# A block-routed expert layer: second matmul in 32x32 blocks, its output turned by VectorE instead of TensorE, and some first loads reordered

## The chip, the core and the metric

The kernel runs on one core of a Trainium2 chip. The core has a matrix engine (TensorE, PE in the profile; its weight loads are the row PEld), a vector engine (VectorE, DVE), a scalar engine (ScalarE, ACT), a general engine (GpSimd, POOL) and SyncE (SP), which here only asks for transfers. Transfers run on 16 DMA engines and are asked for by SP or POOL. Matrix products read SBUF and write PSUM; DVE and ACT read both, and what they copy from PSUM to SBUF is called an eviction here. The metric is device time in microseconds of one execution, the median of several.

## What is computed

`x` and the context are 4 x 1024 x 512, fp32. A layer norm and a cross-attention with 16 heads of 32 are added to `x`; after a second layer norm comes the expert layer, which is the part most touched by the change. Cut to what matters:

```python
grouped = x.reshape(B, g, t, d)                         # 128 groups of t = 32 tokens
logits  = einsum('bgtd,des->bgtes', grouped, controller) + tie   # 32 x 4 = 128 experts
perm    = (logits == max(logits, over t))               # each expert takes one token of a group
dispatched   = einsum('bgtd,bgtes->bgesd', grouped, perm)
inner        = relu(einsum('bgesd,desf->bgesf', dispatched, f1) + bias)   # f = 32
intermediate = einsum('bgesf,esfd->bgesd', inner, f2)   # back to d = 512
out          = einsum('bgesd,bgtes->bgtd', intermediate, perm)
```

So every one of 128 experts has its own 512x32 and 32x512 matrices and sees one token of each of the 128 groups. The second layer is thus 128 small products: 128 groups x 32 hidden times 32 x 512. Its result is needed with the experts on the contraction axis, since the last line sums over experts: for one group, (32 tokens x 128 experts) times (128 experts x 512).

## The kernel before, in words

**Attention** (`attention_phase`, to line 1409) works in 16 units (4 batches x 4 groups of 4 heads). A planner written in Python (`post`, `choose`, `run_engines`, `columns`) gives each piece of work a cost and lays out a fixed order for PE, DVE, ACT, POOL and SP. Before the planner starts, lines 1028 to 1056 issue the first unit by hand: on SP the first 128 columns of the weights for keys, values and queries, the first context and rows, then (lines 1036 to 1042) the other 384 columns of each weight (`load_others`), the output weight (`load_weight("o")`), and the biases `bo_sb` and `bv_sb`. `bv_sb` is spread by a DVE copy (line 1074) that stands in DVE's order ahead of the centring of rows 4 to 7 (line 251).

**First expert layer** (`FirstLayer.dispatch`, line 1457, and `products`, line 1544). For each quarter `c` of the 512 columns, `dispatch` multiplies rows by the 0/1 matrix, so that `disp` holds [128 columns, 128 experts, 128 groups]; `products` multiplies by `f1` and adds into `inner`, which holds [4 experts x 32 hidden, 32 sets of 4 experts, 128 groups]. Weights come in blocks of 512 KB through a pool of four buffers (`load_weights`, `next_weights`): 16 blocks of `f1`, then 16 of `f2`.

**Second expert layer** (from line 1595). The 512 output columns are worked in `DQ` = 4 slices of `DW` = 128. In each slice:

- `second_layer` (line 1612), called for `m` = 0 to 7: 16 products, each of one expert, with `inner` as the stationary operand: 32 hidden x 128 groups, times 32 x 128 of `f2`. Four experts lie on the four groups of 32 partitions and write four PSUM tiles `py`, with the groups on the partitions. Four evictions (line 1608 on DVE, 1610 on ACT) write them into `y` [128 groups, 128 columns, 128 experts].
- `turn` (line 1633), called for `k` = 0 to 31: four 128x128 transposes on PE take a column's [groups, experts] to [experts, groups]; one eviction of each four, DVE and ACT by turns, writes `yT` [128 experts, 128 groups, 128 columns].
- `combine` (line 1650), called for `a` = 0 to 7 in the loop of the following slice, between the products of that slice: 16 products `po` of `permT` (one group's 128 experts x 32 tokens) with `yT`, a DVE addition to the rows of `x` (line 1661), and a store of 256 KB, mostly asked for by POOL.

`permT` (2 MB) is loaded once, the rows of `x` in 32 loads of 256 KB, both on SP. The order of PE, DVE, ACT and SP in this part is that of the program text (`manual_schedule`); an instruction that waits holds up all behind it on its engine.

Of the kernel before, what the change touches and what calls it, by code (L numbers as in the profile page):

```python
# [18 lines left out]
P = 128  # L19
# [13 lines left out]
def attention_phase(  # L33
# [1001 lines left out]
    load_ctx(0, 1)  # L1035
    for key, src in (("q", wqT), ("k", wkT), ("v", wvT)):
        load_others(key, src)
    load_weight("o", woT)
    bo_sb = opool.tile([P, D], F32, tag="bo", name="bo_sb")
# [7 lines left out]
    ln_root(0)  # L1047
    run(v_step(0, 0))
    for t in range(4):
        ln_center(t)  # L1050
# [4 lines left out]
    ln_root(1)  # L1055
    run(q_step(0, 0))
    even = wpool.tile([P, 32], F32, tag="even", name="even")
    nc.gpsimd.memset(even, 1.0 / D)
# [353 lines left out]
class FirstLayer:  # L1412
# [44 lines left out]
    def dispatch(self, c, n, rows, disp, banks=None):  # L1457
        nc = self.tc.nc
        T, G = self.T, self.G
        half, tb = divmod(n, 4)  # L1460
        disp_v = disp[:, :, ts(half, G // 2)].rearrange("p e (r t) -> p r e t", r=4)
        pool, tag = banks or (self.ps_d, "pd")
        pds = [
            pool.tile([P, 4, self.ES], F32, tag=tag, name=f"pd_{c}_{n}_{r}") for r in range(4)
        ]
        for i in range(4):
            for r in range(4):
                nc.tensor.matmul(  # L1468
                    pds[r][:, i, :], lhsT=rows(i)[ts(r, T), :],
                    rhs=self.perms[ts(r, T), 4 * n + i, :], start=True, stop=True,  # L1470
                )
        for r in range(4):
            dst = disp_v[:, r, :, ts(tb, 4)]
            src = pds[r].rearrange("p t e -> p e t")
            if r % 2 == 0:
                nc.vector.tensor_copy(dst, src)
            else:
                nc.scalar.copy(dst, src)
# [3 lines left out]
def ffn_phase(ctx: ExitStack, tc, consts, x2_dram, routed, first_layer, f1, biasT, f2, out):  # L1482
# [25 lines left out]
    wpool = pool(ctx, "ffn_w", 4, side="right")  # L1508
    DQ, NM = f2.shape[0], f2.shape[1]
    DW = D // DQ  # L1510
    weights = deque()

    def load_weights(n):


        w = wpool.tile([P, 8 * P], F32, tag="w", name=f"w_{n}")
        if n < 4 * NC:
            c, k = divmod(n, 4)
            nc.sync.dma_start(w, f1[ts(c, P), ts(k, 8 * P)])
        else:  # L1520
            dq, k = divmod(n - 4 * NC, NM // 2)
            w = w.rearrange("p (m i d) -> p m i d", m=2, i=4)
            nc.sync.dma_start(w, f2[dq, ts(k, 2)].rearrange("m p i d -> p m i d"))
        weights.append(w)

    for n in range(4):
        load_weights(n)
    loads = iter(range(4, 4 * NC + DQ * NM // 2))

# [7 lines left out]
    with first_layer.stack:  # L1537
# [6 lines left out]
        def products(c, disp, f1k, k):  # L1544
            pi = ps_i.tile([P, QB, G], F32, tag="pi", name=f"pi_{c}_{k}")
            for q in range(QB):
                nq = k * QB + q
                for j in range(4):
                    nc.tensor.matmul(  # L1549
                        pi[ts(j, F), q, :],  # L1550
                        lhsT=f1k[:, ds(((k % 2 * QB + q) * 4 + j) * F, F)],
                        rhs=disp[:, 16 * (nq // 4) + 4 * j + nq % 4, :],
                        start=True, stop=True,
                    )
# [40 lines left out]
    with ExitStack() as second:  # L1595
        ytpool = pool(second, "ffn_yT", 1)
        xpool = pool(second, "ffn_x", 8)
        tpool = pool(second, "ffn_permT", 1)
        ypool = pool(second, "ffn_y", 1)
        ps_y = pool(second, "ps_y", 6, space=PSUM)  # L1600
        ps_o = pool(second, "ps_o", 2, space=PSUM)
        permT = tpool.tile([ES, N], F32, tag="permT", name="permT")
        x2_v = x2_dram.rearrange("(a t p) d -> a p t d", p=P, t=4)
        out_v = out.rearrange("(a t p) d -> a p t d", p=P, t=4)

        def evict(on_vector, dst, src):
            if on_vector:
                nc.vector.tensor_copy(dst, src)
            else:
                nc.scalar.copy(dst, src)  # L1610

        def second_layer(dq, m, y):

            f2t = weights[0][:, m % 2]

            banks = [(ps_y, "py")] * 3 + [(ps_o, "po") if dq == 0 else (ps_y, "py")]
            pys = [
                pool.tile([G, 4, DW], F32, tag=tag, name=f"py_{dq}_{m}_{j}")
                for j, (pool, tag) in enumerate(banks)
            ]  # L1620
            for i in range(4):
                for j in range(4):
                    nc.tensor.matmul(  # L1623
                        pys[j][:, i, :], lhsT=inner[ts(j, F), 4 * m + i, :],
                        rhs=f2t[ts(j, F), i, :], start=True, stop=True,
                    )
            for j in range(4):
                evict(
                    j == 0 or (j == 2 and (dq == 0 or m == NM - 1)), y[:, :, ds(16 * m + 4 * j, 4)],
                    pys[j].rearrange("g i d -> g d i"),  # L1630
                )

        def turn(dq, k, y, yT):

            pt = ps_y.tile([ES, 4, G], F32, tag="py", name=f"pt_{dq}_{k}")
            for i in range(4):
                nc.tensor.transpose(pt[:, i, :], y[:, 4 * k + i, :], ident)  # L1637
            evict(k % 2 == 0, yT[:, :, ts(k, 4)], pt.rearrange("e i g -> e g i"))

        xts = deque()  # L1640
        rows = iter([(dq, a) for dq in range(DQ) for a in range(NM)])

# [7 lines left out]
        def combine(dq, a, yT):  # L1650

            xt = xts.popleft()
            po = ps_o.tile([P, 4, DW], F32, tag="po", name=f"po2_{dq}_{a}")
            for i in range(4):
                t = 4 * a + i
                for r in range(4):
                    nc.tensor.matmul(  # L1657
                        po[ts(r, T), i, :], lhsT=permT[:, ds(t * P + r * T, T)],
                        rhs=yT[:, (t // 16) * GH + r * 16 + t % 16, :], start=True, stop=True,
                    )  # L1660
# [3 lines left out]

        yT = None
        with tc.manual_schedule(engines=order):
            for dq in range(DQ + 1):
                before = yT
                if dq < DQ:
                    y = ypool.tile([G, DW, ES], F32, tag="y", name=f"y_{dq}")  # L1670
                for m in range(NM):
                    if dq < DQ:
                        second_layer(dq, m, y)
                        if m % 2 == 1:
                            weights.popleft()
                            next_weights()
                    if dq:
                        combine(dq - 1, m, before)
                        if m < NM - 1:
                            load_x()  # L1680
                    elif m == 1:
                        nc.sync.dma_start(permT, permT_dram)
                if dq < DQ:
                    yT = ytpool.tile([ES, G, DW], F32, tag="yT", name=f"yT_{dq}")
                    for k in range(DW // 4):
                        turn(dq, k, y, yT)
                        if k % 4 == 3 and (dq == 0 or k == 3):
                            load_x()

# [66 lines left out]
```

## Time and profile before

| what | value |
|---|---|
| median of the timed runs | 1349.78 us (1345.71, 1350.24, 1349.78) |
| the profiled execution's own time, its span | 1340.95 us, 1339.2 us |
| granted TensorE clock, mean | 0.992 |
| busy share of the span: PE, PEld, DVE, ACT, POOL | 96%, 50%, 67%, 36%, 37% |
| second expert layer, first `py` product to the end | 1198.6 to 1339.2 us |
| first product `py` (line 1623) to last | 1198.6 to 1309.2 us, 1024 records |
| turns `pt` (line 1637) | 1211.0 to 1324.7 us, 512 records |
| combines `po` (line 1657) | 1230.9 to 1333.4 us, 1024 records |
| DMA in the whole span | 119.59 MB, mean 89 GB/s |

An fp32 product shows as two records of PE, a transpose as one. A group line of the profile reads: line, engine, operation, what it writes <- what it reads, shapes, xcount | busy us, mean ns of one | idle us of its engine just before, and what ended that idle. A timeline line reads: start us, duration us, engine, line, operation, and in brackets the idle before it and its releaser; neighbours of one kind are merged into one line. A window line gives a stretch, its length, the busy time of PE, PEld, DVE, ACT and POOL with counts, the granted clock, the busy share of the DMA engines and GB/s.

### The profile page before, as it was taken

Reading aid. Unit: us, or ns where it says so; the run is one execution under the profiler, and the core shown is the slowest. Engines: PE = TensorE matmul, PEld = TensorE weight load, DVE = VectorE, ACT = ScalarE, POOL = GpSimd, SP = SyncE. Lnnn points to the kernel's source line nnn. Section 1 sums busy time; section 2 is a strip of 40 time slices with the busy share of each in tenths; the row PEclk is TensorE's granted clock in tenths of the full one; section 3 lists DMA queues with packets and bytes.
Section 4 is the critical chain, followed back from the end, with each engine's and each line's share of the span. In section 5 each row is a group of like instructions: output and inputs, shape, how many; then the busy total and the mean of one; then the engine's idle time right before and its main releaser. Section 6 shows DMA issues by size and latency. Waiting matters only on the chain.

```text
span 1339.2 us, 45912 instructions
## 1 busy us (share of the span) xinstructions
PE 1280.7 (96%) x20926; PEld 666.2 (50%) x20926; DVE 891.5 (67%) x1189; ACT 487.1 (36%) x694; POOL 497.1 (37%) x683
## 2 busy tenths in 40 slices
PE   7999999999999999999999999999997999998997
PEld 3533453345344534443434344444532556788887
DVE  5675756766676678566667666676676566776776
ACT  1123333343333333333323233333344234456663
POOL 1036365655242435734252437152564110000211
PEclk9999999999999999999999999999998999998999
DMA  8101202110130211002311010010313776655665
GB/s 291 34 2 59 85 17 69 36 44 14 57 122 27 72 53 54 26 22 79 102 41 53 25 30 12 20 36 26 99 58 108 271 223 200 198 162 189 205 206 144
DMA packets 87730, 119.59 MB, mean 89 GB/s; under 512 B 7128, under 2 KB 48496, under 8 KB 87408
## 3 DMA queue, kind: packets, MB, share of 16 engines
q1 hardware_dynamic: 84656, 107.22, 25.2%
q0 software_dynamic: 2880, 9.44, 2.2%
q8 instruction: 163, 2.67, 0.8%
q14 instruction: 31, 0.25, 0.1%
HBM read 87.33 MB, written 29.31 MB: 87 GB/s over the span
## 4 chain that ended last, share of the span: by engine, by line
PE 81%; DVE 9%; issue 4%; DMA 3%; POOL 1%; SPq 1%; ACT 1%; DVEq 0%; POOLq 0%
PE sc L588 11%; PE pk L27 8%; PE pq L27 8%; PE av L832 8%; PE pv L27 7%; PE st L726 7%; PE po L27 6%; PE pt L1637 4%; PE st L719 3%; PE pd L1468 3%; PE pi L1549 2%; PE po L1657 2%; PE py L1623 2%; PE po L1300 2%; DVE nm L607 2%
## 5 line engine op out<-in xcount | busy, mean ns | idle before, releaser
L735 ACT ACTIVATE pr<-st 128x1024 f32<-128x1024 f32 (+1 forms) x320 | 282.8, 936 | 453.4 <-PE st L726 392.8
L743 POOL TENSOR_SCALAR_AFFINE_SELECT pr<-pr 128x256 f32<-128x256 f32 x256 | 130.0, 525 | 378.5 <-ACT pr L735 372.8
L617 DVE TENSOR_REDUCE nm<-sc 128x2 f32<-128x1024 f32 x192 | 226.1, 1219 | 48.4 <-PE sc L588 27.1
L811 POOL TENSOR_TENSOR acc<-acc,pr 128x256 f32<-128x256 f32 (+3 forms) x122 | 189.6, 1565 | 62.8 <-ACT pr L735 56.1
L811 DVE TENSOR_TENSOR acc<-acc,pr 128x1024 f32<-128x1024 f32 (+3 forms) x128 | 125.9, 998 | 80.8 <-POOL pr L743 48.8
L588 PE MATMUL sc<-kT,qT 32*128 32x512 f32 (+3 forms) x1536 | 170.2, 523 | 0.4 <-DVE qT L423 0.2
L832 PE MATMUL av<-pr,v 128*32 128x512 f32 (+3 forms) x1536 | 158.2, 495 | 5.6 <-POOL pr L743 5.0
L726 PE MATMUL st<-qT,kT 32*128 32x512 f32 (+3 forms) x1536 | 154.9, 489 | 0.0
L27 PE MATMUL pk<-ct,w_k 128*32 128x512 f32 x1024 | 127.4, 609 | 7.5 <-DMA ct<-in_ctxT_dram 6.6
L27 PEld LDWEIGHTS pv<-w_v,ct 128*32 128x32 f32 x4096 | 110.2, 110 | 43.1 <-issue 23.1
L27 PE MATMUL pv<-w_v,ct 128*32 128x128 f32 x4096 | 126.4, 275 | 5.2 <-DVE rd L907 2.8
L27 PE MATMUL pq<-xnT,w_q 128*32 128x512 f32 x1024 | 125.5, 605 | 4.6 <-DVE rd L907 2.2
L607 DVE TENSOR_REDUCE nm<-sc 128x2 f32<-128x256 f32 (+1 forms) x128 | 79.5, 684 | 37.9 <-PE sc L596 37.9
L588 PEld LDWEIGHTS sc<-kT,qT 32*128 32x128 f32 x1536 | 61.5, 185 | 85.4 <-issue 49.5
L27 PE MATMUL po<-w_o,atT 128*32 128x512 f32 x768 | 93.0, 597 | 0.8 <-ACT mxT L389 0.5
L1663 POOL DMA_DIRECT2D out_dram<-xr x28 | 21.1, 753 | 185.4 <-DVE xr L1661 185.4
L832 PEld LDWEIGHTS av<-pr,v 128*32 128x32 f32 x1536 | 40.5, 110 | 81.8 <-issue 65.2
L726 PEld LDWEIGHTS st<-qT,kT 32*128 32x128 f32 x1536 | 71.0, 185 | 11.3
L719 PEld LDWEIGHTS <-ones 32*128 32x128 bf16 x768 | 17.4, 91 | 111.8 <-issue 111.3
L27 PEld LDWEIGHTS pk<-ct,w_k 128*32 128x32 f32 x1024 | 28.5, 110 | 79.9 <-issue 62.7
L719 PE MATMUL st<-mxT,ones 32*128 32x512 bf16 (+3 forms) x768 | 62.0, 329 | 5.2 <-DVE nm L617 4.5
L808 POOL TENSOR_TENSOR acc<-pr,pr 128x768 f32<-128x768 f32 (+1 forms) x24 | 48.5, 2029 | 42.0 <-ACT pr L735 42.0
(124 smaller groups left out, 1544.5 us busy)
## 6 DMA issues: line engine op xcount, KB each, us to landing
w<-in_f_dram SPq DMA_DIRECT2D x32, 512.0 KB, 4.4
xr<-in_x_dram SPq DMA_DIRECT2D x32, 256.0 KB, 2.7
xn_dram<-x SPq DMA_DIRECT2D x8, 1024.0 KB, 5.1
xr<-x_dram SPq DMA_DIRECT2D x32, 256.0 KB, 4.9
inverse<-inverse_dram SPq DMA_DIRECT2D x124, 64.0 KB, 2.3
ct<-in_ctxT_dram SPq DMA_DIRECT2D x7, 1024.0 KB, 5.3
out_dram<-xr POOLq DMA_DIRECT2D x28, 256.0 KB, 4.6
xt<-in_x_dram SPq DMA_DIRECT2D x6, 1024.0 KB, 5.8
```

The source lines that it names most:

```text
L27: nc.tensor.matmul(out[ts(j, 32)], lhsT=lhsT[:, ts(j, 32)], rhs=rhs, start=start, stop=stop)
L588: nc.tensor.matmul(scs[r // 2][:, r % 2, ds(at, n)], lhsT=qT[rr, ts(i, P)], rhs=kT[rr, ds(c0, n)], start=at == 0, stop=last,)
L607: nc.vector.tensor_reduce(nm[:, slot, ts(g, 2)], scs[g][:, :, ds(at, n)], AX.X, ALU.max, negate=True)
L617: nc.vector.tensor_reduce(nm[:, places[0][2], ts(g, 2)], scs[g], AX.X, ALU.max, negate=True)
L719: nc.tensor.matmul(scs[r // 2][:, r % 2, ds(at, n)], lhsT=ones16[rr, :], rhs=mxT[rr, ds(q0, n)], start=at == 0, stop=False,)
L726: nc.tensor.matmul(scs[r // 2][:, r % 2, ds(at, n)], lhsT=kT[rr, ts(j, P)], rhs=qT[rr, ds(h * HS + q0, n)], start=False, stop=at + n == total,
L735: nc.scalar.activation(pr[:, :, :total], scs[g][:, :, :total], AF.Exp)
L743: nc.gpsimd.affine_select(out=d, in_=d, compare_op=ALU.is_ge, fill=0.0, base=0 if places[0][0] == 0 else -1, pattern=[[0, 2], [P + 1, P]], ...
L808: engine.tensor_tensor(acc[:, :, q0:], before[:, :, q0:], part, ALU.add)
L811: engine.tensor_tensor(acc, acc, part, ALU.add)
L832: nc.tensor.matmul(av[rr, q0:], lhsT=vs[u][:, j, rr], rhs=prs[u, k][r // 2][:, r % 2, ds(at, n)], start=(j == 0), stop=last and at + n == ...
L1637: nc.tensor.transpose(pt[:, i, :], y[:, 4 * k + i, :], ident)
```

## The change

1. **Loads at the start.** The other columns of the weights for keys and values and the output weight are asked for after the hand-issued keys and values, and those for queries after the hand-issued queries. In SP's own order this puts `bo_sb` and `bv_sb` directly behind the second half of the context, then the weights k, v, o, q (before: q, k, v, o, `bo_sb`, `bv_sb`).
2. **Order of experts and groups.** The host lays out the controller and `f2` otherwise; `dispatch` and `products` address `disp` accordingly, with the groups in blocks of 32. Shapes and counts there stay.
3. **Second layer.** A round is one slice of 128 columns and one block `b` of 32 groups: 16 rounds. In each of its two halves `second_layer` issues 64 products of 32x32 stationary operands: 32 hidden of one expert x 32 groups. Row group `r` of the partitions (4) and column group `j` (4) give 16 positions. The result has, on each group of 32 partitions, 32 groups of tokens for 8 experts a half, in two tiles `py` of twice the former size; the pool holds three. ACT evicts them into `y` [4 x 32 groups, 32 experts, 128 columns], DVE only two in the first round. Then `turn` lets DVE transpose 32x32 blocks, from `y` to `yT`, both in SBUF, in two instructions of 128 x 64 x 32 a round. `yT` holds [128 experts, 32 groups, 128 columns].
4. **Combine** follows two rounds later (`LAG`) and is spread over the halves, each with 16 products as before.
5. **Transfers.** `f2` comes in the same 16 blocks of 512 KB, each now one piece; the odd slices have a pool of their own (`fpool`), the first of them asked for ahead of the rows of `x`. `permT` is asked for ahead of this part; in SP's order it stands before the last block of `f1`.

```diff
-    for key, src in (("q", wqT), ("k", wkT), ("v", wvT)):
-        load_others(key, src)
-    load_weight("o", woT)
     bo_sb = opool.tile([P, D], F32, tag="bo", name="bo_sb")
...
     run(v_step(0, 0))
+    for key, src in (("k", wkT), ("v", wvT)):
+        load_others(key, src)
+    load_weight("o", woT)
...
     run(q_step(0, 0))
+    load_others("q", wqT)
...
-        half, tb = divmod(n, 4)
-        disp_v = disp[:, :, ts(half, G // 2)].rearrange("p e (r t) -> p r e t", r=4)
+        block, tb = divmod(n, 2)
+        disp_v = disp[:, :, ts(block, T)].rearrange("p e (r t) -> p r e t", r=4)
...
-                        rhs=disp[:, 16 * (nq // 4) + 4 * j + nq % 4, :],
+                        rhs=disp[:, 32 * (nq % 4) + 4 * (nq // 4) + j, :],
...
+        def second_layer(dq, b, half, y):
+
             pys = [
+                ps_y.tile([P, 2, 4, DW], F32, tag="py", name=f"py_{dq}_{b}_{half}_{g}")
+                for g in range(2)
             ]
+            for m in range(4):
+                w = f2s[dq, 2 * half + m // 2]
                 for j in range(4):
+                    for r in range(4):
+                        nc.tensor.matmul(
+                            pys[r // 2][ts(j, T), r % 2, m, :],
+                            lhsT=inner[ts(r, F), 4 * (4 * half + m) + j, ts(b, T)],
+                            rhs=w[ts(r, F), m % 2, j, :], start=True, stop=True,
+                        )
+            for g in range(2):
+                dst = y.rearrange("p (m r) d -> p r m d", r=4)[:, ts(g, 2), ts(half, 4), :]
+                if g and (dq, b) == (0, 0):
+                    nc.vector.tensor_copy(dst, pys[g])
+                else:
+                    nc.scalar.copy(dst, pys[g])
+
+        def turn(part, y, yT):
+            d = ts(part, DW // 2)
+            nc.vector.transpose(
+                yT[:, :, d].rearrange("p g d -> p d g"), y[:, :, d].rearrange("p e d -> p d e")
+            )
...
-                        rhs=yT[:, (t // 16) * GH + r * 16 + t % 16, :], start=True, stop=True,
+                        rhs=yT[:, 8 * r + t % 8, :], start=True, stop=True,
...
+            rounds = [(dq, b) for dq in range(DQ) for b in range(NB)]
+            for n in range(len(rounds) + LAG):
...
+                for half in range(2):
+                    if n < len(rounds):
+                        second_layer(dq, b, half, y)
+                        if b == NB - 1:
+                            for k in range(2):
+                                load_f2(dq + 2, 2 * half + k)
+                    if n >= LAG:
+                        d0, b0 = rounds[n - LAG]
+                        combine(d0, 2 * b0 + half, turned[0])
+                        load_x()
...
+                    for part in range(2):
+                        turn(part, y, yT)
+                    turned.append(yT)
```

## The prediction

> **What bounds the kernel now.** I read the page first (PE busy 96% of a span of 1339.2 us), then the chain of waits, then the stage that the change rewrites, by timeline, groups and windows. The second expert layer runs from the first `py` matmul at 1198.6 us to the end, 140.6 us. The chain of waits of that stage, by line:
>
> ```profile
> by line: PE pt L1637 42.0%; PE po L1657 21.7%; PE py L1623 19.5%; DVE y L1608 8.0%; issue 3.5%; PE pi L1549 0.5%; DVE inner L1560 0.5%; DVE xr L1661 0.5%; ACT yT L1610 0.4%; DVEq L1661 0.0%
> ```
>
> PE's own work is 83% of it (42.0 + 21.7 + 19.5), and half of that is `pt`, the turning by TensorE. The groups of the window from 980 us to the end (count | busy, mean ns | idle before) give what PE pays:
>
> ```profile
> L1637 PE MATMUL pt<-ident,y 128*128 128x128 f32 x512 | 59.3, 280 | 4.2 <-DVE y L1608 2.2 <-issue 2.0
> ...
> L1623 PE MATMUL py<-w,inner 32*128 32x128 f32 x1024 | 38.0, 283 | 1.3 <-DVE inner L1560 1.1
> ...
> L1657 PE MATMUL po<-yT,permT 128*32 128x128 f32 x1024 | 34.3, 275 | 1.4 <-issue 0.7 <-ACT yT L1610 0.7
> ```
>
> So 59.3 us of turns with 4.2 idle, 38.0 of products, 34.3 of combines. In steady state the timeline shows one step of products and one of combine:
>
> ```profile
> 1231.02 0.69 DVE L1608 COPY y<-py 128x512 f32<-128x512 f32 x1 [0.88 <-PE py L1623]
> 1231.05 1.56 ACT L1610 COPY y<-py 128x512 f32<-128x512 f32 x3 [0.58 <-PE py L1623]
> 1231.89 1.17 PE L1623 MATMUL py<-w,inner 32*128 32x128 f32 x32
> 1232.03 0.69 DVE L1661 TENSOR_TENSOR xr<-po,xr 128x512 f32<-128x512 f32 x1 [0.31 <-PE po L1657]
> 1232.99 1.08 PE L1657 MATMUL po<-yT,permT 128*32 128x128 f32 x32
> ...
> 1234.00 1.17 PE L1623 MATMUL py<-w,inner 32*128 32x128 f32 x32
> ```
>
> From product to next product is 2.11 us: 1.10 until the combine starts (32 records 29 ns apart and 0.20 us of change-over), 1.01 for the combine with its change-over. DVE and ACT finish inside it. PE is the bound, except in the turns, where each 0.43 us group waits for an eviction.
>
> **The change, part by part.** *Removed:* 512 transposes (59.3 + 4.2 us of PE), their 128 evictions (44.3 us DVE, 37.5 ACT), and the 512 products of 32x128 (38.0 us).
>
> *Added on PE:* 4 slices x 4 blocks x 2 halves x 64 = 2048 products of 32x32, two records each: 4096, so 128 records a half-round, 32 half-rounds. No 32x32 fp32 product is in the trace. Bounds for the distance between records: below, four times as many tiles overlap, 29/4 = 7.3 ns; above, no more overlap than now, 29 ns. The nearest row for issuing alone is the mask's small products:
>
> ```profile
> 29.17 0.42 PE L596 MATMUL sc<-mask_strict,spots 32*128 32x96 bf16 x28
> ```
>
> 28 products with their weight loads in 0.42 us: 15 ns each, last one's drain included. I take 11 ns, the middle of 7.3 and 15. A half-round is then 128 x 11 = 1.41, plus 0.20 of change-over, 1.01 of combine and 0.3 of waiting (below): 2.92 us; at 7.3 ns 2.44, at 15 ns 3.43, at 29 ns 5.22. [...]
>
> *On ACT:* 64 `y` evictions of 1024 elements, less two that DVE takes, for 128 of 512 (44.5 us ACT, 28.1 DVE). *Added on DVE:* 32 turns of 2048 elements a partition, SBUF to SBUF. Rows for the sizes:
>
> ```profile
> L735 ACT ACTIVATE pr<-st 128x1024 f32<-128x1024 f32 x256 | 248.2, 1021 | 386.9 <-PE st L726 330.9 <-issue 51.6 <-POOL acc L811 4.5
> L617 DVE TENSOR_REDUCE nm<-sc 128x2 f32<-128x1024 f32 x192 | 226.1, 1219 | 48.4 <-PE sc L588 27.1 <-PE sc L596 21.0
> ...
> L1608 DVE COPY yT<-pt 128x512 f32<-128x512 f32 x64 | 44.3, 692 | 16.7 <-PE pt L1637 15.8 <-issue 0.5
> ...
> L1608 DVE COPY y<-py 128x512 f32<-128x512 f32 x43 | 28.1, 687 | 12.1 <-PE py L1623 12.1
> ```
>
> An ACT eviction is 1.02 us, two a half-round: 2.04 of 2.92, hidden. There are three `py` tiles and a half needs two, so the third product of the next half waits for the first eviction: about 1.35 us after the last product, 0.3 more than the combine covers. On DVE 512 elements take 687 ns and 1024 take 1219: 1.04 ns an element and 155 ns fixed, so 2048 take 2.28 us. That holds if the turn runs like a copy. Its elements lie 512 B apart on both sides. The last row above reads single elements 512 B apart in PSUM and pays nothing (687 against 692 ns), but no row reads or writes lone 512 B-spaced elements in SBUF: every strided write now is in runs of four. Bounds: 2.28 us, and twice the element time, 4.41 us, if each element costs a second step; I take 2.28, the row nearest in kind. [...]
>
> *DVE per round* (two halves): 2 x 2.28 + 2 adds x 0.69 + 4 gaps x 0.05 = 6.14 us, against PE 5.84, ACT 4.1. So DVE becomes the bound by a little. Behind a waiting turn on DVE queue only the adds of the round before; PE waits for those through two `po` tiles, a round of slack. `y` has two buffers, `yT` three, so turns run back to back.
>
> *The sum.* The last `f1` product stays at 1198.6. The f2 weights of the first slice are asked for as before, one per 2.1 us from 1192.4, 4.4 us to land: the fourth lands near 1203.3, and the faster products wait for it; y of block 0 is complete near 1205.5. DVE then runs 16 x 6.14 = 98.2, to 1303.7; 0.5 for the last combine's dependence on the last turn; 4.8 from the last add to the end as now (1334.4 to 1339.2): 1309.0. I add 3 us for the first rounds, where the second slice's weights and the first rows arrive together: 1312, so -27.
>
> *Transfers:* counts and sizes stay (16 x 512 KB of f2, x and out 256 KB each), only where they sit changes. The 2 MB of `permT` goes ahead of the last f1 load on SP, under the first layer's last 33.6 us, at 144 GB/s; its cover is that the last f1 block is used 8 us after it is asked for, and a miss costs those few us. From 1203 on 23.1 MB must move, 235 GB/s at the forecast pace. The windows (last columns: DMA share, GB/s):
>
> ```profile
> 1198.60:1211.00 12.40, 9.87 (x258) 8.32 (x256) 10.35 (x17) 9.74 (x18) 0.00 (x0) 1.00 0.79 266
> ...
> 1275.00:1311.00 36.00, 34.87 (x749) 31.20 (x742) 25.59 (x38) 24.04 (x44) 7.52 (x10) 1.00 0.61 196
> ```
>
> 266 was reached; at 196 the transfers would need 118 us and end the kernel near 1321.
>
> *First layer:* the new order of the 128 experts changes offsets only; same shapes, same runs of four: nothing, either way under 1 us.
>
> *Start of the kernel.* The bias loads move ahead of 3.25 MB of weights on SP; those land in the same total time, w_q's last part last.
>
> ```profile
> 29.28 0.43 DVE L1074 COPY bv_rows<-bv_sb 128x512 f32<-128x512 f32 x1 [8.80 <-DMA bv_sb<-in_bv_dram]
> ...
> 31.45 0.69 DVE L389 COPY kT<-pk 128x512 f32<-128x512 f32 x1
> ...
> 32.19 3.70 PE L27 MATMUL pv<-w_v,ct 128*32 128x128 f32 x128 [1.25 <-DVE kT L389]
> ```
>
> DVE stood 8.8 us for `bv_sb`; behind it queue four rows of normalisation, then the eviction of `kT`, and PE's `pv` waits for that. `pk` ends at 28.2, so without the wait the eviction comes at 28.4 and `pv` starts near 30.2, after the mask products and one turn: 2.0 us earlier. PE is the bound from there. Bounds 0 (another wait takes over) and 3 (the eviction's whole gain); I take 2. The later part of w_q, now last, lands near 29 and is first read by the second unit's queries, at 37.6 now.
>
> Together -27 - 2 = -29 us on a profiled execution of 1340.95 (span 1339.2 and 1.75 around it): 1312. The timed runs lie at 1345.71 to 1350.24, median 1349.78, up to 0.7% above the profiled one; forecast on their footing **1321**. Likely case: 7.3 to 15 ns on PE (at 15 PE bounds, 32 x 3.43 = 110 us, -15) and 2.28 to 2.6 us a turn; with either footing 1306 to 1335.
>
> **Rivals.** (1) *The turns cost double.* 4.41 us: a round is 8.82 + 1.38 + 0.20 = 10.4, 16 rounds 166.4, end 1205.5 + 166.4 + 0.5 + 4.8 = 1377, less 2: +36, 1377 on the profile's footing, 1386 on the runs'. It decides from 3.3 us a turn (8.15 us a round). For it: no row with lone strided elements in SBUF. Against: reads at that stride in PSUM are free. (2) *The 32x32 blocks overlap no further than four tiles.* The change does then not do what it says: 32 x 5.22 = 167 us from 1201.3, a tail of 14.4 (evictions 2.1, turns 4.6, combine and adds 2.9, store 4.8): 1383, less 2: +42, 1391. It decides from 19 ns a record. For it: every fp32 row now sits at 26 to 31 ns. Against: these rows have just four tiles, and the 15 ns row. [...] (3) *Transfers set the pace,* under 235 GB/s: at 196, -20, about 1330, inside the likely range.
>
> **How the numbers follow.** Likely case with (3) 0.56, a smaller gain (16 to 18 ns, or turns of 2.7 to 3.1) 0.06; within 0.5%, which is about what a measurement of this kernel can tell from no change, 0.08; (1) and its partial forms 0.19; (2) 0.11. Faster 0.62, same 0.08, slower 0.30. The range runs from 1306 to 1378: it takes in rival 1 on the profile's footing and leaves out its upper half, (2) at full price, and a little below, together under 0.2. The likeliest case alone: 1306 to 1335.
>
> **What would show it.** Turns at 2.3 us and DVE over 90% busy from 1206 on: right; at 4.4: rival 1. 128 `py` records in 0.9 to 1.9 us: right; in 3.7: rival 2. `bv_rows` near 21 us instead of 29.3 and `pv` near 30. ACT evictions near 1.02. I would be wrong if `po` waits for `xr` or `permT` from DMA, or if the first rounds stand for weights longer than 5 us.

## The result and the profile after

The changed kernel takes 1388.78 us (median, 1382.53 to 1391.83) against 1350.01 us (1345.71 to 1352.51) for the kernel before: a ratio of 1.0285, interval 1.0240 to 1.0329. It is slower by 39 us where a gain of 29 was forecast. The profiled execution took 1388.79 us, its span is 1387.1 us at a mean granted clock of 0.976.

The groups of the kernel after, from 1190 us to the end:

```profile
L1646 DVE STREAM_TRANSPOSE yT<-y 128x2048 f32<-128x2048 f32 x32 | 135.0, 4289 | 5.9 <-ACT y L1642 5.8
L1632 PE MATMUL py<-w,inner 32*32 32x128 f32 x4096 | 75.7, 307 | 40.5 <-issue 36.4 <-ACT y L1642 4.1
L1642 ACT COPY y<-py 128x1024 f32<-128x1024 f32 x62 | 59.9, 1016 | 102.3 <-PE py L1632 88.9 <-issue 13.4
L1666 PE MATMUL po<-yT,permT 128*32 128x128 f32 x1024 | 42.8, 306 | 21.4 <-issue 13.8 <-DVE xr L1670 7.4
```

Two rows stand out. A turn takes 4.29 us, not 2.28. And PE stands 36.4 + 13.8 us for "issue", which means that nothing the profile shows ended that idle time. In the kernel before, products and combines lost 1.3 and 1.4 us in all. Both are seen at once in the timeline of the kernel after, in steady state:

```profile
1258.94 8.52 DVE L1646 STREAM_TRANSPOSE yT<-y 128x2048 f32<-128x2048 f32 x2 [0.36 <-ACT y L1642]
1259.97 1.04 PE L1632 MATMUL py<-w,inner 32*32 32x128 f32 x61 [0.88 <-issue]
1260.94 1.08 PE L1666 MATMUL po<-yT,permT 128*32 128x128 f32 x32
...
1261.95 0.73 PE L1632 MATMUL py<-w,inner 32*32 32x128 f32 x35
1263.45 1.46 PE L1632 MATMUL py<-w,inner 32*32 32x128 f32 x93 [0.77 <-issue]
1264.83 1.08 PE L1666 MATMUL po<-yT,permT 128*32 128x128 f32 x32
...
1265.84 0.40 PE L1632 MATMUL py<-w,inner 32*32 32x128 f32 x3
1267.19 1.88 PE L1632 MATMUL py<-w,inner 32*32 32x128 f32 x125 [0.95 <-issue]
1267.32 1.28 DVE L1670 TENSOR_TENSOR xr<-po,xr 128x512 f32<-128x512 f32 x2
1268.49 8.46 DVE L1646 STREAM_TRANSPOSE yT<-y 128x2048 f32<-128x2048 f32 x2
```

DVE goes from turn to addition to turn without a hole: 9.5 us a round here. PE runs, stops, runs. Count the records between its stops: 61 + 32 + 35 = 128, then 93 + 32 + 3 = 128. Each record has a weight load beside it (the page counts 23486 of each), so PE stops every 256 instructions, wherever in the work that falls. The instructions themselves come to the core by a DMA queue of their own, q8 (packets, MB, share of the DMA engines). After:

```profile
q8 instruction: 183, 3.00, 0.9%
```

and before:

```profile
q8 instruction: 163, 2.67, 0.8%
```

Twenty packets more, of 3.00 MB / 183 = 16 KB each. The second layer of the kernel before issues (1024 + 512 + 1024) x 2 = 5120 PE instructions, the new one (4096 + 1024) x 2 = 10240. The difference is 20 x 256. I call one packet a piece. In the trace of the packets the gap before 1263.45 goes with the piece that lands at 1262.20, and the one before 1267.19 with the piece that lands at 1265.96: PE starts again 1.25 and 1.23 us behind the landing.

The forecast's own chain ended at 1310 us of the span; the measured one is 77 us longer. The first turn starts at 1212.7 instead of 1203.5 (+9); from there to the end of the last turn it takes 165.9 us instead of 98.2 (+68, 10.37 us a round instead of 6.14); from the last turn to the end 8.5 instead of 5.3 (+3); the 3 us of allowance fall away. Part of the 9 us is spread between executions: the kernel after and e1 to e3, e5, e7 and e11 below have the same code up to the first `py` product, and it starts anywhere from 1192.0 to 1208.0 us (1206.1 here). So single executions are best compared by the stage alone, from the first `py` product to the end of the span: 140.6 us before, 181.0 after, about 113 in the forecast.

### The profile page after: what moved, and what is told of

It is laid out like the page before. It is cut to its first block, busy times and chain, and to the rows that moved or that the text cites. A ratio compares the mean times of both kernels' runs of the same rounds, so it can differ in the third digit from the quotient of the medians.

```text
span 1387.1 us, 50863 instructions
## 1 busy us (share of the span) xinstructions
PE 1271.3 (92%) x23486; PEld 638.4 (46%) x23486; DVE 954.9 (69%) x1116; ACT 464.8 (34%) x607; POOL 496.0 (36%) x683
## 4 chain that ended last, share of the span: by engine, by line
PE 77%; DVE 9%; issue 8%; DMA 4%; ACT 1%; SPq 1%; POOL 1%; DVEq 0%; POOLq 0%
PE sc L588 10%; PE pk L27 8%; PE pq L27 8%; PE av L832 7%; PE st L726 7%; PE pv L27 7%; PE po L27 6%; PE py L1632 5%; PE po L1666 3%; PE pd L1469 3%; PE st L719 3%; PE pi L1550 2%; DVE nm L607 2%; PE po L1301 2%; DVE rd L907 2%
## 5 line engine op out<-in xcount | busy, mean ns | idle before, releaser
L1646 DVE STREAM_TRANSPOSE yT<-y 128x2048 f32<-128x2048 f32 x32 | 135.0, 4289 | 5.9 <-ACT y L1642 5.8
L1632 PE MATMUL py<-w,inner 32*32 32x128 f32 x4096 | 75.7, 307 | 40.5 <-issue 36.4
L1642 ACT COPY y<-py 128x1024 f32<-128x1024 f32 x62 | 59.9, 1016 | 102.3 <-PE py L1632 88.9
L1632 PEld LDWEIGHTS py<-w,inner 32*32 32x32 f32 x4096 | 53.8, 110 | 60.2 <-issue 48.7
```

Of the source, the lines that this page charges most:

```text
L1632: nc.tensor.matmul(pys[r // 2][ts(j, T), r % 2, m, :], lhsT=inner[ts(r, F), 4 * (4 * half + m) + j, ts(b, T)], rhs=w[ts(r, F), m % 2, j, : ...
L1642: nc.scalar.copy(dst, pys[g])
L1646: nc.vector.transpose(yT[:, :, d].rearrange("p g d -> p d g"), y[:, :, d].rearrange("p e d -> p d e"))
```

## The experiments

**Theory.** Two bounds lie beside each other. The turn pays for elements 512 B apart in SBUF, and PE gets no more than 256 instructions in about 3.8 us. **Rivals:** the turn's length alone; contention of the transfers; PSUM tiles or the clock; a fixed time for each record on PE.

**1. The turn with its elements in a row** (both sides; then on the reading, then on the writing side alone). The blocks that DVE turns are then other ones, so y is not turned as the combine needs it; all counts and sizes stay. The edit of e1; e2 takes only its second new line (reads in a row), e3 only its first (writes in a row):

```diff
...
-                yT[:, :, d].rearrange("p g d -> p d g"), y[:, :, d].rearrange("p e d -> p d e")
+                yT[:, rows, :].rearrange("p g (a d) -> p (g a) d", d=T),
+                y[:, rows, :].rearrange("p e (a d) -> p (e a) d", d=T),
```

> The turn reads and writes 2048 elements in a row on both sides, so that the 32x32 blocks lie elsewhere; the output of the expert layer is therefore left out as a meaningful result, and everything else is as in the changed kernel. Theory (the lone 4-byte elements 512 B apart in SBUF cost a second step): the turn falls from 4.29 us to 2.28, DVE is no longer the bound, and the kernel falls from 1389 to between 1320 and 1345 us. Rival (an fp32 turn takes two steps an element wherever its elements lie): the turn stays at 4.3 us and the kernel within 5 us of 1389.

> Only the read side of the turn lies in a row, the write side stays 512 B apart; the turned layout is left out as in the run before. Theory with the cost on the read side: 2.3 us a turn. With the cost on the write side: 4.3 us. With a share on each: about 3.3 us. Rival (fp32 itself): 4.3 us.

> Only the write side of the turn lies in a row, the read side stays 512 B apart; the turned layout is left out. Theory with the cost on the write side: 2.3 us a turn; on the read side: 4.3 us; a share on each: about 3.3 us. Rival (fp32 itself): 4.3 us.

Measured: e1 1379.67 us (1375.88 to 1382.96), ratio to before 1.0270 [1.0241, 1.0300]; single runs of e2, 1376.88, and e3, 1372.19. The turns, with two later layouts for comparison (ns, shortest / median / longest of 32):

| reads | writes | one turn |
|---|---|---|
| 512 B apart | 512 B apart (the change) | 4107 / 4295 / 4454 |
| in a row | 512 B apart (e2) | 3605 / 3722 / 3805 |
| 512 B apart | in a row (e3) | 3574 / 3726 / 3798 |
| in a row | in a row (e1) | 2268 / 2300 / 2312 |
| in a row | 16 B apart (e13, see 5) | 3734 / 3854 / 4159 |
| in a row | 8 B apart (e14, see 5) | 2249 / 2296 / 2422 |

So the spacing makes the turn slow, either side alone costs 1.42 us, and both together 2.0; e2 and e3 are longer than the 3.3 us that a share on each side was to give. But of 32 x 2.0 = 64 us the kernel gains 4 to 9, and e1 misses the 1320 to 1345 us that its theory gave: it is 34.7 us behind the kernel before run beside it (1344.93), the change 38.8. The stage takes 178.0 us, 3.0 less than in the change. Its groups there:

```profile
L1632 PE MATMUL py<-w,inner 32*32 32x128 f32 x4096 | 76.7, 315 | 38.8 <-issue 34.9 <-ACT y L1642 3.9
L1646 DVE STREAM_TRANSPOSE yT<-y 128x2048 f32<-128x2048 f32 x32 | 72.0, 2287 | 4.5 <-ACT y L1642 4.5
...
L1671 DVE TENSOR_TENSOR xr<-po,xr 128x512 f32<-128x512 f32 x32 | 21.7, 680 | 66.6 <-PE po L1667 66.6
```

Most of the 63 us that the turns gave up stand one row lower: DVE now waits 66.6 us for `po`, 12.1 in the change, and PE's "issue" is as it was. The turn alone as cause falls.

**2. Half and twice the PE instructions.** e5 takes e1 and lets one stationary operand serve two experts, 256 columns a product (the second expert of each pair is then multiplied by the first one's hidden values, so the result is not the layer's); e11 cuts each product into two of 64 columns. Columns, evictions and turns stay. e7 has e5's products with the spaced turn.

```diff
-            for m in range(4):
+            for m in range(0, 4, 2):
...
-                            pys[r // 2][ts(j, T), r % 2, m, :],
+                            pys[r // 2][ts(j, T), r % 2, m : m + 2, :],
...
-                            rhs=w[ts(r, F), m % 2, j, :], start=True, stop=True,
+                            rhs=w[ts(r, F), :, j, :], start=True, stop=True,
```

and for e11:

```diff
+                        for h in range(2):
...
-                            pys[r // 2][ts(j, T), r % 2, m, :],
+                                pys[r // 2][ts(j, T), r % 2, m, ts(h, 64)],
...
-                            rhs=w[ts(r, F), m % 2, j, :], start=True, stop=True,
+                                rhs=w[ts(r, F), m % 2, j, ts(h, 64)], start=True, stop=True,
```

> The flat turn as in e1_turn_flat, and beside it half as many products, each with 256 columns instead of 128: one stationary operand serves two experts, so the second expert of each pair is computed with the first one's hidden values; columns, evictions, turns and transfers stay. Theory A (PE is starved of instructions: in e1_turn_flat its gaps come every 256 instructions and end about 1.3 us after a 16 KB piece of queue q8 has landed, some 3.7 to 4 us apart): the second layer issues 6144 PE instructions instead of 10240, 24 pieces x 3.9 = 94 us, no longer the bound; DVE is, with 16 rounds of 2 x 2.29 + 2 x 0.71 + 0.2 = 6.2 us, 99 us, so the end comes near 1206 + 5 + 99 + 6 = 1316 and the time is 1310 to 1330 us, with py idle ended by issue down from 34.9 us to under 12. Theory B (PE waits for PSUM tiles, transfers or the clock, and the pieces only happen to fall there): the same columns and the same evictions, so 1365 to 1380 us as in e1_turn_flat (1379.67).

> The changed kernel with its 512-byte-spaced turn, and the half as many, 256 column wide products of e5_flat_wide (the second expert of each pair with the first one's hidden values). Takes away the instruction supply as a bound and leaves the slow turn. If both are bounds, each nearly alone enough: DVE's round is 2 x 4.29 + 2 x 0.67 + 0.2 = 10.1 us, 16 rounds 162 us from about 1211, end near 1211 + 162 + 6 = 1379; so 1370 to 1385 us, nearly nothing gained over the changed kernel's 1388, and DVE busy over 95% between 1215 and 1370. If the turn's length is no bound by itself and the instruction supply is all: 1310 to 1330 us.

> The flat turn as in e1_turn_flat, each product cut into two of 64 columns: the same columns, evictions, turns and transfers, but 18432 PE instructions in the second layer instead of 10240. Theory A (a piece of 256 instructions each 3.7 to 3.9 us): 72 pieces, 266 to 281 us from 1206, so 1470 to 1500 us. Theory B (no bound in the supply): 1375 to 1390 us. Theory D (each record costs at least some 13 ns on PE, supply or not): 8192 records x 13 = 106 us and 33 of combines, 1375 to 1400 us.

Measured (single runs): e5 1328.40, e7 1373.66, e11 1497.21 us, each where the theory of two bounds had it. A fixed 13 ns for each record, theory D, gave 1375 to 1400 us for e11 and falls. The four combinations, in brackets the difference to the kernel before as run beside each:

| | 128 columns, 10240 instructions | 256 columns, 6144 |
|---|---|---|
| turn spaced | 1388.78 (+38.8) | 1373.66 (+23.2) |
| turn in a row | 1379.67 (+34.7) | 1328.40 (-22.1) |
| the stage alone, turn spaced | 181.0 | 165.2 |
| the stage alone, turn in a row | 178.0 | 118.7 |

Either edit alone is worth 4 or 16 us, both together 61; the stage alone says 3, 16 and 62. The brackets of e5 and e7 rest on one run of the kernel before (1350.51; 13 runs in a later batch had a median of 1343.88), the stage does not. That is the picture of two bounds of nearly the same height. e5, which has neither, comes within 8 us of the forecast 1321, and its stage within 6 us of the forecast 113. The piece counts follow the instructions to the unit: 163 before, 167 in e5 and e7 (1024 / 256 = 4 more), 183 after and in e1, 215 in e11 (13312 / 256 = 52 more). In the trace the pieces come 3.8 us apart (median, from 1206 us on) in the kernel after and in e1, 3.71 in e11. Half the clock doesn't lengthen this: the trace gives the granted clock in stretches of full and of half speed, and in e11 pieces wholly at full clock come 3.62 us apart (median of 30), wholly at half 3.57 (15); the 27 across a change of clock are longer, 3.89. The products of e5, of e11, and the products and turns of e7:

```profile
L1632 PE MATMUL py<-w,inner 32*32 32x256 f32 x2048 | 58.3, 429 | 15.3 <-issue 10.6 <-ACT y L1642 3.0 <-DMA w<-in_f_dram 1.7
```
```profile
L1633 PE MATMUL py<-w,inner 32*32 32x64 f32 x8192 | 143.2, 251 | 86.6 <-issue 86.5
```
```profile
L1632 PE MATMUL py<-w,inner 32*32 32x256 f32 x2048 | 61.1, 480 | 4.0 <-ACT y L1642 2.9 <-DMA w<-in_f_dram 1.2
L1646 DVE STREAM_TRANSPOSE yT<-y 128x2048 f32<-128x2048 f32 x32 | 135.2, 4311 | 0.1
```

"issue" goes 10.6, 34.9 (e1), 86.5 us with 6144, 10240, 18432 instructions at the same columns. In e7 PE's product row has no "issue" left, and DVE waits 0.1 us before 135.2 us of turns.

**3. Fewer transfers.** e6 is e1 without the loads of the rows of `x` (the combine's result is copied, not added) and without the weights of the last two slices, which use those of the first two.

```diff
-                nc.sync.dma_start(xt, x2_v[a, :, :, ts(dq, DW)])
...
-            nc.vector.tensor_tensor(xt, po, xt, ALU.add)
+            nc.vector.tensor_copy(xt, po)
...
+                if dq > 1:
+                    f2s[dq, k] = f2s[dq - 2, k]
+                    return
```

> The flat turn as in e1_turn_flat, with 12 of the second layer's some 23 MB of transfers left out: the rows of x aren't loaded (the combine's result is copied instead of added to them), and the last two slices use the weights of the first two. Products, evictions, turns and stores stay. Theory A1 (a piece of instructions takes its time for itself, whatever else moves): 1365 to 1380 us, gaps on PE still every 256 instructions. Theory A2 (the pieces come late because they stand in line with the other transfers): the gaps shrink by half or more, time 1325 to 1355 us. Theory C (the data transfers themselves are the bound): time falls to under 1340 us and the gaps no longer keep to 256 instructions.

Measured: 1364.30 us, just under the range of theory A1. The gaps stay at 128 records, and the median distance of the pieces is 3.75 us; the mean falls from 4.13 (e1) to 3.79. So the other transfers delay some pieces, 40 x 0.34 = 14 us in all (the stage fell by 15, from 178.0 to 162.8), but a piece takes its 3.75 us without them.

**4. The start, and permT.** e4 is the kernel before with the first loads reordered as in the change, and nothing else. e8 is the changed kernel with `permT` asked for behind the second slice's weights:

```diff
-        nc.sync.dma_start(permT, permT_dram)
         x2_v = x2_dram.rearrange("(a t p) d -> a p t d", p=P, t=4)
...
                     load_f2(dq, k)
+            nc.sync.dma_start(permT, permT_dram)
```

> The kernel before with the reordered first loads alone. Forecast by the prediction: the bias copy no longer waits until 29 us, pv starts 2 to 3.7 us earlier (32.2 to about 28.5), and the kernel is 2 to 4 us faster than 1350. Rival (the planner's later waits take it back): pv earlier all the same, the kernel within 1.5 us of before.

> The changed kernel with the 2 MB load of permT asked for behind the weights of the second slice instead of ahead of the last block of the first layer's weights; nothing else. Theory: the last block of f1 comes 2 to 5 us sooner, the wait before the last pi products (1.95 us now) falls under 1 us and the first py product starts 2 to 3 us sooner relative to the first layer's start; the whole time changes by -1 to -4 us, little beside the run to run spread, 1383 to 1389. Rival: the later start of py comes from the lower clock and other order in the first layer, and permT costs nothing or would now be missed by the first combine: 1387 to 1395, with po waiting for permT.

Measured: e4 1340.10 us, ratio 0.9958 [0.9937, 0.9978], 3 to 8 us faster; e8 (single run) 1388.61, no change. In the kernel after, the rows that were shown of before at 29.28 and 32.19 us are at 20.42 (`bv_rows`) and here (`pv`):

```profile
28.50 3.70 PE L27 MATMUL pv<-w_v,ct 128*32 128x128 f32 x128
```

In the profiled execution of e8 the first layer (`pi`) ends sooner than in that of the kernel after, and PE then stands in the next gaps:

```profile
1196.14 3.57 PE L1550 MATMUL pi<-disp,w 128*32 128x128 f32 x121 [0.74 <-issue]
1199.65 0.41 PE L1631 MATMUL py<-w,inner 32*32 32x128 f32 x6
1203.15 1.95 PE L1631 MATMUL py<-w,inner 32*32 32x128 f32 x126 [3.09 <-issue]
```

The kernel after has that `pi` row at 1200.93 (5.24 us long, 1.95 of "issue" before it, at a granted clock of 0.83 from 1196 to 1206), and its first `py` at 1206.10. But e1 to e3, which ask for `permT` where the change does, have their first `py` at 1192.0 to 1197.7, so the sooner end isn't shown to come from `permT`; and the first turn is at 1212.7 in the kernel after and at 1213.8 in e8. These runs show no effect of the place of `permT` on the end.

**5. Layouts that could be used.** e9 is the changed kernel with `y` and `yT` as [columns, 32], so that ACT writes runs of eight experts (their order changes with the controller's columns) and the combine reads `yT` 128 B apart. e10 has in addition slices of 256 columns, and asks for `permT` behind the first slice's weights. e12 spreads e10's combines over all four quarters of a round. e13 and e14 are e12 and write `yT` 16 and 8 B apart, so that PE reads runs of 16 and 8 B.

```diff
-                dst = y.rearrange("p (m r) d -> p r m d", r=4)[:, ts(g, 2), ts(half, 4), :]
+                dst = y[:, :, ts(2 * half + g, 8)]
+                src = pys[g].rearrange("p r m d -> p d (r m)")
...
-                yT[:, :, d].rearrange("p g d -> p d g"), y[:, :, d].rearrange("p e d -> p d e")
+            nc.vector.transpose(yT[:, d, :], y[:, d, :])
...
-                        rhs=yT[:, 8 * r + t % 8, :], start=True, stop=True,
+                        rhs=yT[:, :, 8 * r + t % 8], start=True, stop=True,
```

e10, beside this (a tile `w` now holds 256 columns of `f2` for one `m`; the two halves of the columns have tiles `y` and `yT` of their own), and e12's combine of one `a` at a time:

```diff
-        "f2": a["ffn_f2"].reshape(4, 2, 4, 128, 4, 128).transpose(4, 0, 3, 1, 2, 5),
+        "f2": a["ffn_f2"].reshape(8, 4, 128, 2, 256).transpose(3, 0, 2, 1, 4),
...
-                            rhs=w[ts(r, F), m % 2, j, :], start=True, stop=True,
+                            rhs=w[ts(r, F), j, :], start=True, stop=True,
...
-                    if n and q % 2 == 1:
+                    if q == 0:
+                        if 0 <= n - 2 < R:
+                            step(n - 2, 1, 1)()
+                    elif 0 <= n - 1 < R:
+                        done = step(n - 1, (q - 1) // 2, (q - 1) % 2)
```

e14 against e12 (in e13 the 2 is a 4 and `HW // 4` is `HW // 8`):

```diff
-                nc.vector.transpose(yT[:, d, :], y[:, d, :])
+                nc.vector.transpose(
+                    yT[:, ts(part, HW // 4)].rearrange("p d g i -> p d i g"),
+                    y[:, d, :].rearrange("p (d i) e -> p d i e", i=2),
...
-                        rhs=yT[:, :, 8 * r + t % 8], start=True, stop=True,
+                        rhs=yT[:, :, 8 * r + t % 8, :], start=True, stop=True,
```

> The changed kernel with the turn's elements in a row on both sides by another layout, the output whole: ACT writes y as [column, expert] in runs of eight experts (their order in a block changes with the controller's columns), the turn reads and writes in a row, and the combine's products read yT with a spacing of 128 bytes. Products are still 128 columns wide. Theory A: turns of 2.29 us, ACT evictions unchanged (1.02 us) since the writes are in runs, and the instruction supply the bound as in e1_turn_flat: 1370 to 1382 us. Rival: PE's reads or ACT's writes pay for the spacing: po records longer than 330 ns or y evictions longer than 1.2 us, and 1385 to 1420 us.

> A version that takes away both bounds with the output whole: e9's layout, and slices of 256 columns, so that a product of 32x32 streams 256 columns and the second layer issues 6144 PE instructions instead of 10240; y and yT in tiles of half a slice, evictions of 512 elements, permT asked for behind the first slice's weights. Theory A: DVE is the bound, 8 rounds of 4 x 2.29 + 4 x 0.70 + 0.3 = 12.3 us, 98 us, from a first turn near 1214 (eight blocks of weights instead of four come first), plus 7 us to the end: span 1319 to 1332, faster than before (1350) by 1 to 2.5%. Rival: the combine's spaced reads or the more evictions (128 of 0.55 us on ACT) make a new bound: 1340 to 1375 us, with DVE idle over 25% between 1220 and 1310.

> As e10_flat_wide, with the two combines of a half slice spread over two quarters: one group of 32 po records behind each quarter's products instead of 64 behind every second. In e10_flat_wide PE needed 7.7 us for two quarters: 1.69 + 0.95 of waiting for an eviction + 1.46 + 3.68 for 64 po records of 57 ns (they read yT at 128 bytes' spacing; 29 ns in the kernel before). If the wait for the PSUM tile goes behind the combine: 4 x (1.6 + 1.84) = 13.8 us a round instead of 15.5, 8 rounds save 14 us: span 1320 to 1328, ratio to before 0.983 to 0.993. Rival: the wait only moves (adds behind turns hold the po tiles): 1333 to 1342 and PE waits for xr instead.

> [...] If only large spacings cost: turns under 2.6 us, po records near 30 ns, DVE bound at 12.3 us a round, 1312 to 1325. If PE pays for anything but a row: po records stay above 50 ns.

> [...] If any spacing costs in full: turns of 3.6 to 3.8 us and 1350 to 1365. If only large spacings cost: turns under 2.6 us, 1312 to 1325.

Measured: e9 1379.58 us (single run), as e1, and ACT's evictions stay at 1015 ns. Its `po` records are already the rival's, 395 ns instead of 273 (medians, e1 the second), but at 10240 instructions this hides behind the pieces. e10 1345.60, ratio 1.0030 [1.0009, 1.0050], so its forecast failed and its rival held: with fewer instructions the spaced reads of PE come to the fore, and PE waits 17.3 us for ACT's evictions besides. Two `po` groups in its timeline, each 64 records:

```profile
1263.63 3.68 PE L1665 MATMUL po<-yT,permT 128*32 128x128 f32 x64
...
1271.46 3.67 PE L1665 MATMUL po<-yT,permT 128*32 128x128 f32 x64
```

That is 57 ns a record, where the kernel before had 32 in 1.08 us, 34. e12: 1343.47, ratio 1.0019 [0.9994, 1.0045]; the wait only moved, as its rival had it (PE waits 16.2 us for `xr`). e13 1396.33, e14 1340.53 us (single runs). Their `po` and turn rows, e13 first (shortest / median / longest ns):

```profile
L1666 PE MATMUL po<-yT,permT x1024: 272/419/424, 1227.4 to 1389.5; 128*32 128x128 f32 x171
L1645 DVE STREAM_TRANSPOSE yT<-y x32: 3734/3854/4159, 1219.8 to 1380.2; 128x2048 f32<-128x2048 f32 x32
```
```profile
L1666 PE MATMUL po<-yT,permT x1024: 269/272/422, 1223.3 to 1333.0; 128*32 128x128 f32 x171
L1645 DVE STREAM_TRANSPOSE yT<-y x32: 2249/2296/2422, 1218.0 to 1325.8; 128x2048 f32<-128x2048 f32 x32
```

A write to every fourth element costs DVE about as much as one 512 B away (3.85 us a turn against 3.72); a write to every second element costs nothing (2.30, as in a row). So "only large spacings cost" fails with the turn of e13 and "any spacing costs in full" with that of e14. In e13 PE besides waited 60.8 us for additions behind the long turns; e14's time is 16 us over the 1312 to 1325 that were to go with turns under 2.6 us, for the reason in 6. PE reads runs of 8 B in 272 ns a record, as rows in the kernel after (273, medians); in e13, with runs of 16 B, 586 of the 605 `po` records that start at half clock take over 340 ns, and 8 of the 419 at full clock, where groups of 32 in 1.08 us are found too.

**6. Both bounds away.** In e14 an addition stood behind a turn on DVE and held the `po` tile that PE needed. e15 puts it ahead:

```diff
                     if q == 0:
                         if 0 <= n - 2 < R:
                             step(n - 2, 1, 1)()
+                        if 0 <= n - 1 < R:
+                            yTs[n - 1, 1] = ytpool.tile(
...
+                            turn(old, yTs[n - 1, 1])
...
-                    turn(ys[1], yTs[n, 1])
+                old = ys[1]
```

> As e14_runs_of_2 (turn writes at 8 bytes' spacing for 2.30 us, PE reads runs of 8 bytes for 29 ns a record, output whole), with the second turn pair of a round put behind the first addition of the next round on DVE, so that PE no longer waits for a po tile whose addition queues behind a turn. e14 took 15.0 us a round, with DVE busy 11.8 of it. If that wait was the rest: DVE's and PE's own work allow 12.5 us, and the supply of PE instructions, 3 pieces a round at 4.4 us as in e14, 13.2; so 8 rounds save 14 to 20 us and the span comes to 1319 to 1326, ratio to before 0.980 to 0.990. If there is a third bound (transfers, weights late, PSUM tiles): 1333 to 1342, ratio 0.993 to 1.0.

Measured: 1333.03 us (1323.67 to 1335.94) against 1348.06 (1340.46 to 1350.85), ratio 0.9884 [0.9850, 0.9918]. This version is faster than both kernels, by 1.2% against before (e4 alone: 0.4%). PE's waiting for `xr` ahead of `po` fell from 22.6 us in e14 to 9.4. The ratio is in the forecast range; the span is 1330.2 us, 8.5 less than e14's and 4 more than forecast. The stage fell by 13.5 us, from 137.2 to 123.7, just under the 14 to 20 forecast; it began 5 us later than in e14. The first turn starts at 1220.3 and the last at 1319.0, so the eight rounds of this layout took 12.6 us each.

## Why the prediction failed

- **The first step that failed is the price of a turn:** "I take 2.28, the row nearest in kind". It measured 4.29 us, near the upper bound of 4.41 that was set beside it. The row taken read single elements 512 B apart in PSUM; it said nothing of SBUF. Nor did the two rows compare spaced with unspaced reads: the 692 ns set beside the 687 are the eviction of `pt`, which reads PSUM 512 B apart as well. That such reads are free in PSUM is shown by the copies to `kT`, which read 512 elements in a row in 692 ns, no less.
- **Rival 1** had the slow turn (4.41 us, measured 4.29) and the round (10.4 us, measured 10.37), and it and its partial forms got a chance of 0.19. That its end came so close (1386, measured 1388.78) is luck in part: in the profiled execution it gave 1377 against 1388.79. The later first turn and the longer end make up that difference, and the 9 us added for the timed runs happened to cover most of it.
- **The price of the spacing in SBUF** stood in no row of before; the runs gave it. Writes 16 B apart cost a turn 1.55 us (3.85 in e13, 2.30 in e1), 512 B apart on one side 1.42 (e2, e3), and 8 B apart nothing (2.30 in e14).
- **The second step that failed is PE's half-round,** put at 2.92 us from a record distance of 11 ns: the supply of PE instructions was not in the sum at all. A half-round has 320 PE instructions, 1.25 pieces, 4.75 us at 3.8 us a piece. So the right price of a turn would not have mended the picture: with the turn at the forecast 2.29 us e1 still took 1379.67. The prediction counted records to price them, but not to ask where they come from.
- **Products of 32x32.** Between two stops 93 records take 1.46 us and 125 take 1.88. That is 15 to 16 ns with the drain, as the row at line 596 had it, and 13 from start to start: at the upper end of the range named as "right". So rival 2 was wrong, the blocks do overlap further than four tiles (13 ns against 29); that a half-round took about its 5.22 us all the same (10.37 a round) has another cause.
- **ACT's evictions** took 1.02 us, as forecast.
- **Start.** Forecast -2 us with bounds 0 and 3; `pv` moved by 3.7 to 4.0 us and e4 gained 3 to 8. The mechanism held, the size was too small.
- **permT.** Whether "a miss costs those few us" is not shown: the first product moves by more than that from execution to execution, and moving `permT` away (e8) moved the end by nothing.
- **What stays open:** why a piece takes 3.75 us. In the trace of the kernel after, from 1206 us on, PE runs some 1.2 us before the packet of the next piece starts, the packet takes 1.04 us, and PE starts 1.4 us after it has landed (medians); what sets these steps no run here varied. And what the granted clock took of the loss; it is the first number behind the five busy times with their counts in the windows of the kernel after:

```profile
1212.00:1240.00 28.00, 18.17 (x768) 13.16 (x769) 23.08 (x9) 9.93 (x11) 1.52 (x2) 0.76 0.50 148
1240.00:1300.00 60.00, 40.68 (x1765) 29.73 (x1771) 52.57 (x24) 21.20 (x22) 8.23 (x11) 0.87 0.58 173
1300.00:1360.00 60.00, 39.42 (x1958) 29.35 (x1956) 58.19 (x26) 23.14 (x24) 8.97 (x12) 0.99 0.32 92
```

In the windows of before it was 0.83 from 1211 to 1231 us, 1.00 from there to 1325 and 0.96 to the end. The part of the lower clock in the loss was not separated; but pieces at half clock come no later than at full (experiment 2), and e5 had 0.75 from 1215 to 1240 and 0.91 to 1300, and reached 1328 all the same. In the last two windows DVE is busy 52.57 and 58.19 us of 60: it is the tighter bound there, the pieces are close behind.

## What to carry to other kernels

Ask of each strided access which memory it is in and how far apart its elements lie: in SBUF the turn's writes were free 8 B apart here and cost DVE 0.7 to 0.8 ns an element 16 or 512 B apart, and a layout with pairs served the turn (2.30 us) and the product behind it (272 ns a record) at once (e14). Where a change makes operations smaller, divide its count of PE instructions, weight loads included, by 256 and hold that many times the 3.8 us measured here against the stage: 128 records with their weight loads in 3.8 us are one in 30 ns, however well they overlap. And try two suspected bounds alone and together, because of two equal ones each looks innocent when only it is removed.

## What the runs showed of the hardware that was not expected

- PE can be starved of instructions by plain straight code. They came in packets of 16 KB, one for 256 of them. In the second layer before, at 29 ns a record, products and combines lost 1.3 and 1.4 us in all; at 13 between stops, 35 to 87 us of idle time ahead of the products were the price (after, e1, e11).
- PE's streamed operand pays too: lone elements 128 B apart nearly doubled its time a record (57 ns against some 30, e10), pairs of 8 B did not (median record 272 ns in e14, 395 in e10).
- One spaced side costs the turn 1.42 us (e2, e3), the second only another 0.57 (after).
